# Interleaving the second attention, and spreading recurrence, routing and row sums over the first, in a four-block transformer kernel

## The chip, the cores and the metric

The kernel runs on one core of one Trainium2 chip. The metric is the device time of one execution in microseconds (us), lower is better. A core has five engines with a program order of their own: PE (TensorE: matmul, with its weight loads as PEld), DVE (VectorE), ACT (ScalarE), POOL (GpSimd) and SP (SyncE); they wait for one another through semaphores. SBUF is the on-chip memory, PSUM the eight banks of 128 x 512 f32 into which PE writes.

## The reference, cut to what matters

X holds 32 sequences of 128 tokens of width 128. Two layers of four sub-blocks run over it; all arithmetic that matters here is f32.

```python
# layer 0
h = x * modulation(cond)                       # modulated
x = x + attention(h, 16 heads of 64, causal) @ W_out
F, I = sigmoid(x @ W_f), sigmoid(x @ W_i)      # recurrence
C = x @ W_h + b_h
f, i = F / (F + I + eps), I / (F + I + eps)
F = scan_t(f * state + i * C)
for cyc in range(3):                           # twist
    th = (0.3*a*tanh-ish gate(F)) + 0.7*a*gate_of_mean
    F = F + th * twist(F)                      # twist(F): F's four quarters permuted, signs changed
x = x + F
# layer 1
gate  = top2(softmax(segment_means(x) ...))    # routed
x = x + experts picked by gate, and a shared one
x = layernorm(x + attention(x, 16 heads of 8, key mask, causal))
x = x + slots(lowrank(x))
```

The two attentions are softmax(Q K^T + mask) V for every sequence and head. The gate th is the same for all 128 rows of one token, so twist(F + th * twist(F)) = twist(F) + th * twist(twist(F)) and twist(twist(F)) = -F.

## The kernel before, in words

X stays in SBUF, transposed (width on the partitions, 4096 token columns), in eight chunks g of 512 columns (CB = 4 sequences of S = 128). `ps()` takes one of the eight PSUM banks, `mm` (L268), `tt` (L279) and `act` (L339) issue a matmul, a two-input elementwise operation on the engine named, and an activation; many groups of the profile therefore carry these helpers' lines and are told apart by their tiles. PE and ACT execute in the order of the program text. For DVE and POOL a list scheduler decides the order.

**First stage (up to about 650 us).** The loop `for h in range(NH + 1)` runs over 16 half-chunks (8 heads of a chunk each) and, inside, over four sequences b. Every (h, b) is one *unit*, pushed on `pipe = Staggered(0, 3, 4, 5)`: on each push the scores of this unit, the transposes of the unit three pushes back, the values of the one four back and, for the last sequence, the output projection of the one five back are issued.

- `scores` (L408 to L434): mask and Q K^T for 8 heads into two banks; a DVE maximum for each bank (L426), 8 exponentials on ACT into `s_sb`, a DVE sum over 128 x 1024 (L431, `s_sum`), its reciprocal (L432), and the normalisation of `s_sb` on POOL (L279).
- `turned` (transposes L441; copies `pT` on ACT and on DVE L443), `values` (copy `oT` on DVE L453), `projected` (adds to X on DVE).

Between the pushes stand, in program order: three pieces of `projections(h + 1)` for each b (Q, K and V of the next half-chunk); `modulated(g + 1)` ahead of the first push of odd h (xs on POOL, one matmul, `hT` on DVE); `recurrence(g)`, all of it after the push at b = 0 of odd h from 3; `twisted(g0, cyc)` after the push at b = 0 of h = 6, 7, 8, 10, 11, 12, 14, 15, 16 (one cycle each of a pair of chunks, in four steps with a projection piece or a push between them); `routed(g0)`, driven to its end at once after the push at b = 3 of h = 8 and 12; and `prepared()`, low-rank and constant preparation for the last sub-block, ahead of the twist at h = 6.

- `recurrence` (L457 to L497): three matmuls with X; F and I by sigmoid on ACT, C on DVE (L480); R = 1 / (F + I + eps) on DVE (L481, L482); products on DVE and POOL; L486; eight scans (L490, L491), POOL product, one scan of 512 columns (L495).
- `twisted` (L500 to L572): three small matmuls with Gelu, then in `fourth` tanh on ACT, L563 on DVE, the matmul `twist` x F, th * twist on DVE, F + th on DVE for the first chunk and on POOL for the second; in cycle 2 X + F on POOL.
- `routed` (L575 to L646): sums of X over segments (DVE), gate matmuls, softmax and top-2 as a chain of some 25 small DVE operations and one exponential on ACT, ending in `r_wd` (L279), a matmul with ones, and the expert rows for the gathers.

**Second stage (about 650 to 1301 us), and a drain.** Four turns r of 32 pieces: 24 expert pieces, then eight attention pushes (two chunks). A dictionary `plan` ties other steps to piece numbers: `last_recurrence` at 2, the twist of the last pair of chunks at 7, 13 and 19, `routed(4)` at 24 and `routed(6)` at 26 of turn 0, and the slot sub-block of the turn before. Expert weights are gathered by indirect DMAs issued from POOL (L786). One attention push issues, through `pipe = Staggered(0, 1, 2, 3, 4)`, in this order: scores(n), weights(n-1), turned(n-2), values(n-3), normed(n-4). For one sequence `weights` are four DVE maxima (L862) and 16 exponentials `s` on ACT for four banks of four heads (hg = 0 to 3), `turned` are 16 transposes (L873) with one copy `p1T` per bank, on DVE (L877) for hg = 0 and 2 and on ACT for 1 and 3, and `values` are 16 matmuls and an ACT copy `oS`.

Of the kernel before, what the change touches and what calls it, by code (L numbers as in the profile page):

```python
# [11 lines left out]
F32 = mybir.dt.float32  # L12
# [227 lines left out]
def program(ctx, tc, out, xT, packs, where):  # L240
# [102 lines left out]
    with (  # L343
# [62 lines left out]
        def unit(h, b):  # L406
# [8 lines left out]
            def scores():  # L415
                two = [ps(), ps()]
                for par in range(2):
                    mm(two[par], ident16, outer(causal16, 4), stop=False)
                for i in range(4):
                    for par in range(2):  # L420
                        r = slice(64 * par, 64 * par + 64)
                        mm(two[par][:, bass.ts(i, S)], qks[h][2 * i][r, cs], qks[h][2 * i + 1][r, cs], start=False, stop=(i == 3))
                s = pool.tile([P, 8, S], F32, tag="s_sb", name="s_sb", bufs=5)
                nm = pool.tile([P, 8], F32, tag="s_max", name="s_max", bufs=5)
                for par in range(2):
                    V.tensor_reduce(nm[:, 4 * par : 4 * par + 4], b3(two[par]), AX.X, ALU.max, negate=True)  # L426
# [4 lines left out]
                V.tensor_reduce(sm, s, AX.X, ALU.add)  # L431
                V.reciprocal(sm, sm)  # L432
                tt(G, s, s, inner(sm, S), ALU.mult)
                at["s"] = s  # L434
# [32 lines left out]
        def recurrence(g, three):  # L467
# [11 lines left out]
            mm(p, w("w_h"), col(g))  # L479
            V.tensor_scalar(C, p, w("b_h"), None, ALU.add)  # L480
            V.scalar_tensor_tensor(R, F, 1e-8, I, ALU.add, ALU.add)  # L481
            V.reciprocal(R, R)  # L482
            tt(V, F, F, R, ALU.mult)
            tt(G, I, I, R, ALU.mult)
            tt(G, I, I, C, ALU.mult)
            V.tensor_scalar(F, F, 1e-8, None, ALU.add)  # L486

            for b in range(CB):
# [4 lines left out]
                )  # L493
            tt(G, I, I, R, ALU.mult)
            V.tensor_tensor_scan(F, w("reset"), I, 0.0, ALU.mult, ALU.add)  # L495
            tt(V, F, F, C, ALU.add)
            Fs[g] = F  # L497


        def twisted(g0, cyc):  # L500

# [52 lines left out]
            def fourth():  # L554
# [4 lines left out]
                for k, g in enumerate(gs):  # L559
                    th = mpool.tile([P, CH], F32, tag="th", name="th")  # L560
                    act(th, two[k], AF.Tanh, bias=hb4, scale=0.5)
                    cB = cBs[g0][:, k * CB : (k + 1) * CB]
                    V.scalar_tensor_tensor(b3(th), b3(th), ar3, inner(cB, S), ALU.mult, ALU.add)  # L563
                    p = ps()
                    mm(p, w("twist"), Fs[g])
                    tt(V, th, th, p, ALU.mult)
                    tt(G if k else V, Fs[g], Fs[g], th, ALU.add)
                    if cyc == 2:
                        tt(G, col(g), col(g), Fs[g], ALU.add)
# [7 lines left out]
        def routed(g0):  # L577
# [14 lines left out]
            V.tensor_scalar(agg[:, 0, :], agg[:, 0, :], 1.0 / S, None, ALU.mult)  # L592
            V.tensor_scalar(agg[:, 1:3, :], agg[:, 1:3, :], 1.0 / (S - LH), None, ALU.mult)
            p = ps()
            for k in range(3):
# [42 lines left out]
            wd = rt([nb, 4, nb], "wd")  # L638
            tt(V, wd, inner(pick, nb), outer(ident[:nb, :nb], 4), ALU.mult)
            p = ps()  # L640
            mm(p[:, : 4 * nb], ones[:nb, :], wd.rearrange("p e b -> p (e b)"))
# [71 lines left out]
        for piece in projections(0):  # L713
            piece()
        pipe = Staggered(0, 3, 4, 5)
        for h in range(NH + 1):


            pieces = []
            if h + 1 < NH:  # L720
                if h % 2:
                    modulated(h // 2 + 1)
                pieces = projections(h + 1)
# [27 lines left out]
    with tc.tile_pool(name="l1", bufs=1) as pool:  # L751
# [87 lines left out]
        def attention(g, b):  # L839
# [16 lines left out]

            def weights():
                four = at["p"]
                s = pool.tile([P, 16, S], F32, tag="s1", name="s1", bufs=2)
                nm = pool.tile([P, 16], F32, tag="s1max", name="s1max", bufs=2)  # L860
                for hg in range(4):
                    V.tensor_reduce(nm[:, bass.ts(hg, 4)], b3(four[hg]), AX.X, ALU.max, negate=True)  # L862
                    for j in range(4):
                        h = 4 * hg + j
                        act(s[:, h, :], four[hg][:, bass.ts(j, S)], AF.Exp, bias=nm[:, h : h + 1])
                at["s"] = s

            def turned():
                pT = pool.tile([P, 16, S], F32, tag="p1T", name="p1T", bufs=2)
                for hg in range(4):  # L870
                    p = ps()
                    for j in range(4):
                        T.transpose(p[:, bass.ts(j, S)], at["s"][:, 4 * hg + j, :], ident)  # L873
                    if hg % 2:
                        act(pT[:, bass.ts(hg, 4)], b3(p), AF.Copy)
                    else:
                        V.tensor_copy(pT[:, bass.ts(hg, 4)], b3(p))  # L877
                at["pT"] = pT

# [273 lines left out]
        def last_recurrence():  # L1153
            three = [pool.tile([P, CH], F32, tag=t, name="rec", bufs=2) for t in ("qT", "kT", "R")]
            recurrence(NCH - 1, three)

# [15 lines left out]
        at(26, routed, NCH - 2)  # L1172
        steps_of = {}

        def twisted_steps(cyc):
            if cyc not in steps_of:
                steps_of[cyc] = twisted(NCH - 2, cyc)
            return steps_of[cyc]

        for r in range(NP):  # L1180
# [18 lines left out]
            at(t + 30, slots_told, c)  # L1199
        pipe = Staggered(0, 1, 2, 3, 4)  # L1200
        running = []
        for i in range(END + 2 * TURN):
# [7 lines left out]
            if k < 3 and 1 <= r <= NP:  # L1210
                pipe.push()
            for gen in list(running):
# [6 lines left out]
            if k >= 24 and r < NP:  # L1219
                b = k - 24  # L1220
                pipe.push(*attention(2 * r + b // CB, b % CB))
                if k == TURN - 1:
                    pipe.push()

# [29 lines left out]
```

## Time and profile before

| what | value |
|---|---|
| three runs of before | 1384.09, 1378.07, 1384.84 us; median 1384.09 |
| the profiled execution | 1384.86 us, of which the span of the trace is 1383.1 |
| mean granted TensorE clock | 0.943 |
| PE busy, first attention (40 to 640 us) | 554.75 of 600 us |
| PE busy, second stage (778 to 1301 us) | 468.15 of 523 us |
| PE busy, drain (1301 to 1383 us) | 52.90 of 82 us, clock 0.66 |
| largest group on POOL | s_sb normalisation, 64 x 1917 ns |
| ACT_TABLE_LOAD | 59 x 1283 ns |

The page gives, for one execution, how long each engine was busy, the span in 40 slices (a digit 9 means busy for 90% or more; PEclk is the granted TensorE clock in tenths), and groups of equal instructions with their number, busy time, mean duration and the idle time ahead of them with the engine and tile that ended it. A timeline line has start, length, engine, line, operation, `out<-in` by tile name, shapes and number; a bracket at its end is the engine's idle time before it and what ended it. Matmuls are pipelined, so a busy PE isn't a PE at its peak. An f32 matmul appears as two records.

### The profile page before, as it was taken

To read this page: it belongs to the slowest core of one execution; us is meant where nothing else is said; L and a number is where in the kernel's file an instruction comes from. 1 tells how busy PE (TensorE), PEld (TensorE's weight loads), DVE (VectorE), ACT (ScalarE), POOL (GpSimd) and SP (SyncE) were. 2 spreads that over 40 slices of the span, in tenths; PEclk is the share of its full clock that TensorE was granted. 3 is DMA by queue.
4 is the path that set the end of the run, shared out by engine and by line. 5 is a ranking of instruction groups with operands and counts; after the bars stand their busy time and mean duration, and the time that the engine had idled before them with its cause. 6 is when DMAs were issued, how large, how long until landed. Compare 5 with 4: busy or idle time off the path is not lost. (4 is left out here: it accounts for less than half of the span.)

```text
span 1383.1 us, 20674 instructions
## 1 busy us (share of the span) xinstructions
PE 1206.7 (87%) x7743; PEld 720.2 (52%) x7743; DVE 784.5 (57%) x1862; ACT 782.7 (57%) x2044; POOL 334.0 (24%) x292
## 2 busy tenths in 40 slices
PE   4999999997999979978788789899899889989856
PEld 1565655444554545544445356655567456665633
DVE  1657684666757567574423764466644755456743
ACT  2765654654565645642554674668546774658521
POOL 1323231322322223222433111321023110311000
PEclk9999999998999999998999799999999999999975
DMA  6000000000000000000424002320044001310000
GB/s 241 1 1 1 1 1 0 1 1 1 1 1 1 1 1 1 1 1 0 155 69 127 12 1 70 120 87 1 9 146 128 11 1 50 121 35 1 12 5 16
DMA packets 15987, 49.67 MB, mean 36 GB/s; under 512 B 1424, under 2 KB 5648, under 8 KB 15504
## 3 DMA queue, kind: packets, MB, share of 16 engines
q0 software_dynamic: 9504, 40.01, 9.1%
q1 hardware_dynamic: 5808, 7.29, 1.5%
q8 instruction: 61, 1.00, 0.3%
q10 hardware_dynamic: 576, 1.05, 0.2%
q14 instruction: 38, 0.31, 0.1%
HBM read 46.25 MB, written 2.10 MB: 35 GB/s over the span
## 5 line engine op out<-in xcount | busy, mean ns | idle before, releaser
L339 ACT ACTIVATE s_sb<-ps,s_max 128x128 f32<-128x128 f32 x512 | 139.2, 383 | 127.1 <-DVE s_max L426 123.8
L279 POOL TENSOR_TENSOR s_sb<-s_sb,s_sum 128x1024 f32<-128x1024 f32 x64 | 122.7, 1917 | 275.2 <-DVE s_sum L432 183.3
L268 PE MATMUL ps<-hT,w_attn 128*128 128x512 f32 x256 | 128.9, 627 | 16.3 <-DVE hT L279 11.8
L339 ACT ACTIVATE s<-ps,s1max 128x128 f32<-128x128 f32 x512 | 134.2, 404 | 1.0 <-DVE s1max L862 1.0
L426 DVE TENSOR_REDUCE s_max<-ps 128x4 f32<-128x512 f32 x128 | 82.2, 680 | 68.0 <-PE ps L268 67.8
L339 ACT ACTIVATE he<-ps,ew 128x128 f32<-128x128 f32 x256 | 72.6, 369 | 63.3 <-issue 29.1
L862 DVE TENSOR_REDUCE s1max<-ps 128x4 f32<-128x512 f32 x128 | 81.8, 681 | 36.2 <-PE ps L268 36.1
L339 ACT ACT_TABLE_LOAD x59 | 75.7, 1283 | 44.5 <-PE ps L268 23.5
L339 ACT ACTIVATE qk<-ps 128x512 f32<-128x512 f32 x128 | 74.8, 627 | 42.3 <-PE ps L268 41.7
L786 POOL DMA_INDIRECT ew<-in_expert,rows x64 | 62.7, 980 | 136.3 <-DVE ye L796 131.3
L431 DVE TENSOR_REDUCE s_sum<-s_sb 128x8 f32<-128x1024 f32 x64 | 77.8, 1216 | 23.7 <-ACT s_sb L339 23.6
L268 PE MATMUL ps<-he,ew 128*128 128x128 f32 x512 | 79.1, 294 | 13.6 <-ACT he L339 11.0
L268 PEld LDWEIGHTS ps<-he,ew 128*128 128x128 f32 x512 | 68.8, 195 | 31.4 <-ACT he L339 29.1
L796 DVE SCALAR_TENSOR_TENSOR ye<-ps,ew 128x128 f32<-128x128 f32 x64 | 22.4, 350 | 107.2 <-PE ps L268 107.2
L268 PEld LDWEIGHTS ps<-hT,w_attn 128*128 128x128 f32 x256 | 45.2, 193 | 69.9 <-issue 40.3
L268 PEld LDWEIGHTS ps<-qk 64*128 64x128 f32 x1024 | 64.6, 194 | 31.4 <-issue 31.4
L268 PE MATMUL ps<-qk 64*128 64x128 f32 x1024 | 77.2, 292 | 0.0
L873 PEld LDWEIGHTS ps<-w_base,s 128*128 128x128 f32 x512 | 59.8, 149 | 32.6 <-ACT s L339 20.4
L873 PE MATMUL ps<-w_base,s 128*128 128x128 f32 x512 | 71.6, 290 | 4.2 <-ACT s L339 4.2
L268 PE MATMUL ps<-pT,v 128*64 128x128 f32 x1024 | 72.5, 285 | 3.0 <-DVE pT L443 2.1
L441 PE MATMUL ps<-w_base,s_sb 128*128 128x128 f32 x512 | 72.1, 285 | 2.8 <-DVE th L279 1.7
L268 PE MATMUL ps<-X,ew 128*128 128x128 f32 x512 | 70.9, 278 | 0.0
(295 smaller groups left out, 2286.9 us busy)
## 6 DMA issues: line engine op xcount, KB each, us to landing
w_attn<-in_attn POOLq DMA_DIRECT2D x2, 1024.0 KB, 10.5
out_x<-ot SPq DMA_DIRECT2D x8, 256.0 KB, 2.3
X<-in_xT ACTq DMA_DIRECT2D x4, 256.0 KB, 7.4
X<-in_xT SPq DMA_DIRECT2D x4, 256.0 KB, 9.5
w_lowr<-in_lowr SPq DMA_DIRECT2D x1, 1024.0 KB, 12.5
ew<-in_expert,rows POOLq DMA_INDIRECT x64, 4.5
w_ffn<-in_ffn SPq DMA_DIRECT2D x1, 928.0 KB, 10.4
w_mix<-in_mix SPq DMA_DIRECT2D x1, 800.0 KB, 11.5
```

The costliest lines, as they stand in the source:

```text
L268: T.matmul(out_, lhsT=lhsT, rhs=rhs, start=start, stop=stop)
L279: eng.tensor_tensor(out_, a, b, op)
L339: return tc.keep_in_program_order(A.activation(*args, **kwargs))
L426: V.tensor_reduce(nm[:, 4 * par : 4 * par + 4], b3(two[par]), AX.X, ALU.max, negate=True)
L431: V.tensor_reduce(sm, s, AX.X, ALU.add)
L441: T.transpose(p[:, bass.ts(i, S)], at["s"][:, 4 * par + i, :], ident)
L786: G.indirect_dma_start(ew, None, table, bass.IndirectOffsetOnAxis(ap=rows[:, r, k : k + 1], axis=0))
L796: V.scalar_tensor_tensor(t, y, ew[:, 1028:1029], ew[:, 1029:EW], ALU.add, ALU.mult)
L862: V.tensor_reduce(nm[:, bass.ts(hg, 4)], b3(four[hg]), AX.X, ALU.max, negate=True)
L873: T.transpose(p[:, bass.ts(j, S)], at["s"][:, 4 * hg + j, :], ident)
```

## The change: what it does

1. *Row sums* (L431): POOL adds the two halves of each row of 128 (128 x 512), then the two quarters of that (128 x 256), and DVE sums what is left (32 columns per head, 256 in all, for 1024).
2. *Recurrence in steps*: `recurrence` becomes a generator of five parts; it is begun after the push at b = 1 (was 0), and each later push runs one part. C is an ACT Identity with bias (was DVE). The reciprocal is taken in two halves.
3. *Twist carried along*: the matmul `twist` x F is issued in cycle 0 only. For the cycles after, `turned[k]` holds twist(F), updated as twist(F) - th * F: the product v on POOL, the subtraction on DVE in cycle 0 and on POOL in cycle 1. The twist steps begin at b = 2 (was 0).
4. *Routing in steps*: three more yields in `routed`, and in the first stage one part is run per push, from b = 3 of h = 8 and 12.
5. *Moved*: `prepared()` from h = 6, b = 0 to h = 16, b = 2; `modulated(g + 1)` from ahead of odd h to after the first push of the even h before it.
6. *Second attention*: `weights` and `turned` take the bank hg as argument, and one push issues, for hg = 0 to 3, weights(n-1, hg) and turned(n-2, hg), then values(n-3), scores(n), normed(n-4). In turn 0 the two carried tiles lie in a tile of `s1`.

```diff
-                V.tensor_reduce(sm, s, AX.X, ALU.add)
+                half = pool.tile([P, 8, 64], F32, tag="s_half", name="s_half")
+                tt(G, half, s[:, :, 0:64], s[:, :, 64:128], ALU.add)
+                tt(G, half[:, :, 0:32], half[:, :, 0:32], half[:, :, 32:64], ALU.add)
+                V.tensor_reduce(sm, half[:, :, 0:32], AX.X, ALU.add)
...
-            V.tensor_scalar(C, p, w("b_h"), None, ALU.add)
+            act(C, p, AF.Identity, bias=w("b_h"))
+            yield
             V.scalar_tensor_tensor(R, F, 1e-8, I, ALU.add, ALU.add)
-            V.reciprocal(R, R)
+            for k in range(2):
+                V.reciprocal(R[:, bass.ts(k, CH // 2)], R[:, bass.ts(k, CH // 2)])
+            yield
...
-                    p = ps()
-                    mm(p, w("twist"), Fs[g])
-                    tt(V, th, th, p, ALU.mult)
-                    tt(G if k else V, Fs[g], Fs[g], th, ALU.add)
+                    F, TF = Fs[g], turned[k]
+                    if cyc == 0:
+                        p = ps()
+                        mm(p, w("twist"), F)
+                        TF = p
+                    if cyc < 2:
+                        v = mpool.tile([P, CH], F32, tag="h1", name="v")
+                        tt(G, v, th, F, ALU.mult)
+                    tt(V, th, th, TF, ALU.mult)
+                    tt(G if k else V, F, F, th, ALU.add)
+                    if cyc < 2:
+                        tt(V if cyc == 0 else G, turned[k], TF, v, ALU.subtract)
...
-                if h % 2:
-                    modulated(h // 2 + 1)
...
-                if b == 0 and 3 <= h < NH and h % 2 == 1:
-                    recurrence((h - 3) // 2, [pool.tile([P, CH], F32, tag="rec%d" % i, name="rec", bufs=1) for i in range(3)])
+                for gen in list(running):
+                    if next(gen, gen) is gen:
+                        running.remove(gen)
+                if b == 1 and 3 <= h < NH and h % 2 == 1:
+                    gen = recurrence((h - 3) // 2, [pool.tile([P, CH], F32, tag="rec%d" % i, name="rec", bufs=1) for i in range(3)])
+                    next(gen)
+                    running.append(gen)
+                if b == 0 and h % 2 == 0 and h + 2 < NH:
+                    modulated(h // 2 + 1)
...
-                if b == 0 and k >= 0 and k % 4 < 3:
-                    if k == 0:
+                if b == 2 and k >= 0 and k % 4 < 3:
+                    if k % 4 == 0:
+                        turned = [pool.tile([P, CH], F32, tag="tw%d" % i, name="tw", bufs=1) for i in range(2)]
+                    work = twisted(2 * (k // 4), k % 4, turned)
+                    if h == NH:
                         prepared()
-                    work = twisted(2 * (k // 4), k % 4)
                 if b == 3 and 0 <= k < NH - 6 and k % 4 == 2:
-                    for _ in routed(2 * (k // 4)):
-                        pass
+                    running.append(routed(2 * (k // 4)))
...
-        pipe = Staggered(0, 1, 2, 3, 4)
+        def advance(item=None):
+            line.append(item)
+            w1, t1, v1, n1 = (line[-k] if k <= len(line) else None for k in (2, 3, 4, 5))
+            for hg in range(4):
+                if w1:
+                    w1[1](hg)
+                if t1:
+                    t1[2](hg)
+            if v1:
+                v1[3]()
+            if item:
+                item[0]()
+            if n1:
+                n1[4]()
```

More of the change, by code (lines that the diff above doesn't have):

```diff
@@ L486, in recurrence @@
             V.tensor_scalar(F, F, 1e-8, None, ALU.add)
+            yield
             for b in range(CB):
@@ L494, in recurrence @@
             tt(G, I, I, R, ALU.mult)
+            yield
             V.tensor_tensor_scan(F, w("reset"), I, 0.0, ALU.mult, ALU.add)
@@ L497, in recurrence, with twisted @@
             Fs[g] = F
-        def twisted(g0, cyc):
+        def twisted(g0, cyc, turned):
             gs = (g0, g0 + 1)
@@ L593, in routed @@
             V.tensor_scalar(agg[:, 1:3, :], agg[:, 1:3, :], 1.0 / (S - LH), None, ALU.mult)
+            yield
             p = ps()
@@ L639, in routed @@
             tt(V, wd, inner(pick, nb), outer(ident[:nb, :nb], 4), ALU.mult)
+            yield
+            yield
             p = ps()
@@ L715, in program @@
         pipe = Staggered(0, 3, 4, 5)
+        turned = {}
+        running = []
         for h in range(NH + 1):
-            pieces = []
-            if h + 1 < NH:
-                if h % 2:
-                    modulated(h // 2 + 1)
-                pieces = projections(h + 1)
+            pieces = projections(h + 1) if h + 1 < NH else []
             for b in range(CB):
@@ L855, in scores, with weights, turned @@
                 at["p"] = four
[L857 to L878, printed above, removed]
+            def weights(hg):
+                p = at["p"][hg]
+                if hg == 0:
+                    at["s"] = pool.tile([P, 16, S], F32, tag="s1", name="s1", bufs=2)
+                    at["nm"] = pool.tile([P, 16], F32, tag="s1max", name="s1max", bufs=2)
+                V.tensor_reduce(at["nm"][:, bass.ts(hg, 4)], b3(p), AX.X, ALU.max, negate=True)
+                for j in range(4):
+                    h = 4 * hg + j
+                    act(at["s"][:, h, :], p[:, bass.ts(j, S)], AF.Exp, bias=at["nm"][:, h : h + 1])
+            def turned(hg):
+                if hg == 0:
+                    at["pT"] = pool.tile([P, 16, S], F32, tag="p1T", name="p1T", bufs=2)
+                p = ps()
+                for j in range(4):
+                    T.transpose(p[:, bass.ts(j, S)], at["s"][:, 4 * hg + j, :], ident)
+                if hg % 2:
+                    act(at["pT"][:, bass.ts(hg, 4)], b3(p), AF.Copy)
+                else:
+                    V.tensor_copy(at["pT"][:, bass.ts(hg, 4)], b3(p))
             def values():
@@ L1154, in last_recurrence @@
             three = [pool.tile([P, CH], F32, tag=t, name="rec", bufs=2) for t in ("qT", "kT", "R")]
-            recurrence(NCH - 1, three)
+            return recurrence(NCH - 1, three)
         TURN, NP = 24 + 2 * CB, NCH // 2
@@ L1172, in program @@
         at(26, routed, NCH - 2)
-        steps_of = {}
+        steps_of, last_turned = {}, []
         def twisted_steps(cyc):
+            if cyc == 0 and cyc not in steps_of:
+                t = pool.tile([P, 16, S], F32, tag="s1", name="tw", bufs=2).rearrange("p h s -> p (h s)")
+                last_turned.extend([t[:, 0:CH], t[:, CH : 2 * CH]])
             if cyc not in steps_of:
-                steps_of[cyc] = twisted(NCH - 2, cyc)
+                steps_of[cyc] = twisted(NCH - 2, cyc, last_turned)
             return steps_of[cyc]
@@ L1199, in program @@
             at(t + 30, slots_told, c)
-        pipe = Staggered(0, 1, 2, 3, 4)
+        line = []
+        def advance(item=None):
[12 more added lines that the diff above has]
+                n1[4]()
         running = []
@@ L1210, in program @@
             if k < 3 and 1 <= r <= NP:
-                pipe.push()
+                advance()
             for gen in list(running):
@@ L1220, in program @@
                 b = k - 24
-                pipe.push(*attention(2 * r + b // CB, b % CB))
+                advance(attention(2 * r + b // CB, b % CB))
                 if k == TURN - 1:
-                    pipe.push()
+                    advance()
 def build(inputs):
```

## The prediction

> **What bounds the kernel now.** I read the page first: engine shares, then busy tenths in 40 slices.
>
> ```profile
> span 1383.1 us, 20674 instructions
> PE 1206.7 (87%) x7743; PEld 720.2 (52%) x7743; DVE 784.5 (57%) x1862; ACT 782.7 (57%) x2044; POOL 334.0 (24%) x292
> ...
> PE   4999999997999979978788789899899889989856
> ...
> PEclk9999999998999999998999799999999999999975
> ```
>
> TensorE is busy for 87% and near full in most slices, so time can be won in three ways only: fewer matmuls, fewer PE stalls, or fewer stretches at the half clock. The stretches of busy time (columns: length; PE, PEld, DVE, ACT, POOL busy; granted clock; DMA) say where the room is.
>
> ```profile
> 40.00:640.00 600.00, 554.75 (x3395) 306.73 (x3392) 387.63 (x638) 347.55 (x854) 176.44 (x104) 0.96 0.00 1
> 336.00:342.00 6.00, 2.24 (x4) 1.33 (x5) 3.28 (x23) 0.20 (x1) 0.26 (x1) 0.50 0.01 3
> 914.00:974.00 60.00, 53.90 (x468) 29.64 (x470) 41.20 (x86) 46.79 (x155) 10.57 (x12) 1.00 0.01 2
> ```
>
> In the first attention (40 to 640) PE lacks 45 us of 600; POOL, with 176 us, has room. 914 to 974 is one block of second attention, with PE busy for 54 us of 60. Next, a plain unit of the first attention in the timeline, since every unit's row sums change:
>
> ```profile
> 154.98 1.29 DVE L426 TENSOR_REDUCE s_max<-ps 128x4 f32<-128x512 f32 x2 [3.41 <-PE ps L268]
> 155.77 2.17 ACT L339 ACTIVATE s_sb<-ps,s_max 128x128 f32<-128x128 f32 x8 [1.71 <-DVE s_max L426]
> ...
> 157.97 1.22 DVE L431 TENSOR_REDUCE s_sum<-s_sb 128x8 f32<-128x1024 f32 x1 [0.23 <-ACT s_sb L339]
> ...
> 159.22 0.20 DVE L432 RECIPROCAL s_sum<-s_sum 128x8 f32<-128x8 f32 x1
> ...
> 159.96 1.90 POOL L279 TENSOR_TENSOR s_sb<-s_sb,s_sum 128x1024 f32<-128x1024 f32 x1 [8.24 <-PE ps L268]
> ...
> 161.33 0.69 DVE L426 TENSOR_REDUCE s_max<-ps 128x4 f32<-128x512 f32 x1 [1.90 <-PE ps L268]
> ```
>
> The mask matmuls of neighbouring units stand at 153.26 and 159.61: one unit is 6.35 us with PE back to back, and DVE waits for PE (3.41 and 1.90 us). The stalls lie in the units that carry more. The waits of PE and the timeline name them:
>
> ```profile
> PE ps L268 <- DVE r_wd L279: 21.4, 4, 7.7
> ...
> PE ps L268 <- DVE th L279: 6.0, 5, 1.9
> ...
> PE ps L268 <- DVE X L279: 5.2, 6, 0.9
> ```
>
> ```profile
> 339.76 0.60 PE L268 MATMUL ps<-r_wd,w_base 8*128 8x32 f32 x2 [7.72 <-DVE r_wd L279]
> ```
>
> Routing stalls PE for 7.72 us twice in the first attention and 5.73 us once in turn 0; the recurrence waits 0.87 us six times for the add to X. Last, one step of the second attention on ACT:
>
> ```profile
> 1101.62 4.22 ACT L339 ACTIVATE s<-ps,s1max 128x128 f32<-128x128 f32 x16
> 1105.61 0.72 ACT L339 ACTIVATE p1T<-ps 128x512 f32<-128x512 f32 x1
> 1106.59 0.60 ACT L339 ACTIVATE p1T<-ps 128x512 f32<-128x512 f32 x1 [0.26 <-PE ps L873]
> 1107.63 0.60 ACT L339 ACTIVATE oS<-ps 128x512 f32<-128x512 f32 x1 [0.44 <-PE ps L268]
> ```
>
> ACT works 6.1 us of a step of about 7 (16 exponentials, two copies, one copy of values) and sits idle for 0.7 us between its copies, behind transposes that stand after all the exponentials.
>
> **What the Trainium skill says.** "TensorE: Matmul & The Clock Gate", What's actually happening: the PE clock falls to half after an idle window of about 3.4 us. The trace agrees: clock 0.50 in 336 to 342, in the 7.72 us stall. "GPSIMD Engine Reference", 3.1 Elementwise: a GpSimd tensor_tensor of 2048 columns takes 4497 ns, so 512 would be near 1.1 us; this trace has 1.27 us (X<-X,F, 128x512), which I use. The same page, 8. Key points: GpSimd shares an SBUF interface with VectorE. The trace's F<-F,th add (1265/1593/1657 ns at minimum, median and maximum) fits such contention, and I let a half sum cost 1.27 to 1.65.
>
> **The change, part by part**, against the profiled run: 1384.86 us, 1.8 outside the span, 0.8 above the median of 1384.09.
>
> 1. *Twist carried along.* 16 of 24 twist matmuls go. Each is two records of 0.43 us spacing (two passes of 512 columns), so 0.86 us on a full PE: 16 × 0.86 = 13.7; 12 lie in the first attention (−10.3), 4 in turn 0, where PE has gaps (−2 instead of −3.4). Added: per pair two v products and a cycle-1 subtraction on POOL for each chunk (1.27 to 1.65 each), cycle-0 subtractions on DVE (0.69). None feeds the next PE step but through F+th, so 0, except in point 6.
>
> 2. *Routing in steps.* The 7.72 us stalls go twice (−15.4). After each, the clock stays at half up to 348, clock 0.84 in 342 to 348; estimate 2.5 us per stall, so −5. Turn 0: −5.7. Next late is the agg reduction, two units of work earlier: nothing. Sum −20 and −6.
>
> 3. *Recurrence from b = 1, in steps.* Its matmuls no longer stand behind the X add of the same push: 0.87 × 6 = −5, and 0.7 more where I see its twin (1.11 us at 134) → −6. C goes to ACT (8 × 0.69), where ACT's share is 58% of this stretch: 0.
>
> 4. *Modulated early; twist away from recurrence.* Units at odd h, b = 2 take 8.6 us against 6.35 + 0.86 for the modulated matmul: 1.4 × 4 = 5.6. Units h = 7 and 11, b = 1 (twist meets recurrence) take 10.05 and 9.97 against 7.2: 5.6. The stalls at h = 15 (1.49, 1.68, 1.07) may remain; −12 with 1 of these. With fewer stalls, fewer half-clock windows: those at 231, 293, 385, 460, 515, 552 are 30 us, cost up to 15; I take −6 (0 to −12).
>
> 5. *prepared moved.* Unit h = 6, b = 0 takes 26.2 us against 17.7 for a twist unit: −8.5. At h = 16 its 32 matmuls (3.76 us) and its ah and xab waits (0.38, 1.26) return in a stretch with stalls: +7.5. Net −1. It issues no DMA; on POOL and SP nothing moves past it.
>
> 6. *Row sums halved on POOL.* Per unit DVE loses 1.22 − 0.41 (estimate from 0.68 for 512 elements) = 0.8, 51 us over 64 units, all beside PE: 0. POOL gains 1.27 to 1.65 (half) and 0.7 to 0.9 (quarter, estimate: half the columns plus its fixed part). The DVE reduction now waits for POOL, and behind it stands the next s_max. In the unit shown: exponentials end 157.94, + 0.05 + 1.35 + 0.75 + 0.1 → 160.2, reduction and reciprocal to 160.9, s_max due at 161.33: 0.4 us of cover. With the upper ends it is 0.2 us late, and twist units have DVE filled (cycle 0 has 3 us more). Bounds 0 and +25 (64 × 0.4); a gain is excluded only while DVE has 1.9 us idle. I take +8.
>
> First attention: −10.3 − 20 − 6 − 12 − 6 − 1 + 8 = −47.
>
> 7. *Second attention interleaved.* Transposes of an older step stand between exponentials, so ACT's copies find them done: the 0.26 + 0.44 us go, and PE's waits for p1T (9.4 us in all) with them. A step then has ACT's 6.1 + 0.2. Before: the first six steps of a block are 6.27 to 7.53 us apart, mean 6.83; so −0.5 × 32 = −16; the loop exponentials, values, masks, maximum (I add these to 6.3) leaves no more. Turn ends see other limits; I take −14, bounds 0 and −25. Cover lost: values(n) wait for group 1's exponentials in the same push through a PSUM bank.
>
> 8. *POOL in turn 0*: v, subtraction and F add (1.3 to 1.65 each) stand between issues of expert gathers (0.98 us each): 8 × 1.5 = 12 us on POOL, busy 43 of 118. Bounds 0 and +6; I take +2. Three more table loads (page count of 59 at 1.28 us): "ScalarE: Activation LUTs", What ACT_TABLE_LOAD costs, gives about 1.28 too: +3.8 of ACT beside PE, 0.
>
> Second stage: −2 − 6 − 14 + 2 = −20. Sum −67: 1384.9 − 67 = **1318 us**.
>
> **The rivals.** (a) *DVE waits for POOL eat the gain*: point 6 at its upper end (+25) and no clock gain (4): −67 + 17 + 6 = −44, and routing's tail still late in part (+4): about 1345. For: POOL's latency stands in DVE's queue. Against: 1.9 us of DVE idle per unit. (b) *Interleave gives nothing*: the new PSUM wait replaces the old: −67 + 14 → 1332; with 0.2 us more per step, 1338. For: exponentials of the next push still depend on scores behind values. (c) *More gain*: steps at 6.1 us (−24 in point 7), half clock gone (−12), 6 at 0: −67 − 10 − 6 − 8 → 1294. (d) *Slower*: POOL becomes the bound of the first attention. Its loop per unit is half + quarter + the reduction's round trip + normalise = 1.65 + 0.9 + 0.9 + 1.9 = 5.35 us, if POOL takes the units strictly one after the other; it decides from 6.35. Were the halves, which read with a stride, to take 3 and 1.9 us, the loop is 7.7 to 8: 1.65 × 64 = +105 − 67 → 1422. Against: 1.27 us is measured for the same number of elements. (e) *The change doesn't act*, since DVE and POOL order is a scheduler's: the built order shows the transposes between exponentials and the routing steps between units; only point 6's placement is open.
>
> **Chances.** Forecast 1318 (1300 to 1335): 0.52; (b) and (a), 1332 to 1365: 0.24; (c) 0.13; between 1365 and 1377: 0.02; within 0.5% (1377 to 1391), which is about what a measurement can tell from no change: 0.03; (d) 0.06. The range takes (a), (b) and most of (c): 1282 to 1362. Faster 0.91, same 0.03, slower 0.06.
>
> **What would show it.** Right: no PE wait for r_wd near 7 us; 4657 instead of 4673 matmul instructions in the program and 64 F,w_mix records for 96; plain units still at 6.35; no clock of 0.50 at the former routing; steps of the second attention at 6.3; half sums at 1.3 to 1.65 us. Wrong: s_max waiting for s_sum or POOL in each unit; half sums above 2 us; ACT idle in second attention with waits on PE values; a PE wait for ah or xab over 3 us at the end of the first attention.

## The result, and the profile after

The changed kernel takes 1376.74 us (median of 19 runs, 1370.38 to 1380.87), the kernel before 1383.65 (19 runs, 1377.44 to 1388.80): a ratio of 0.9952, 95% interval 0.9936 to 0.9969. The forecast was 1318 with a range from 1282 to 1362. The change is worth 7 us, not 67, and the time lies outside the range. The profiled execution spans 1375.8 us.

The page of after, engine shares and the slices of PE, POOL and the clock:

```profile
span 1375.8 us, 20779 instructions
...
PE 1190.6 (87%) x7711; PEld 721.4 (52%) x7711; DVE 759.2 (55%) x1870; ACT 782.6 (57%) x2055; POOL 495.4 (36%) x444
...
PE   4999898979898998977787889898899989998865
...
POOL 1655655465555555552544311221023110311100
PEclk9999999989999899978899999999999899999876
```

PE did lose 16 us of busy time (1206.7 to 1190.6), and DVE 25, but the span fell by 7.3 only, and POOL went from 334 to 495 us. PE stands still elsewhere: its waits in after are

```profile
PE ps L268 <- ACT h L339: 28.1, 19, 8.3
...
PE ps L268 <- DVE pT L446: 13.9, 5, 3.6
```

The wait for r_wd (21.4 us before) is gone from this list, as forecast, and that for X fell from 5.2 to 0.4. In its place PE waits 28.1 us for the twist's h (8.2 before) and 13.9 for pT (2.8 before). Both stand behind the softmax maxima: h behind exponentials on ACT, these behind s_max on DVE, and pT behind s_max on DVE itself. At 282.83 us, for instance, PE has stood still for 4.69 us: ACT waits 4.34 us for s_max, loads a function table (1.28 us), does the exponentials and one copy, loads a table again (1.28 us), and only then forms h. Two stretches show where the time went, the first attention up to the scores of its last unit, and from there to the first scores of the second attention. (The columns are those of the stretches shown for before.) After:

```profile
40.00:613.00 573.00, 528.01 (x3240) 291.02 (x3239) 348.88 (x617) 341.41 (x845) 316.58 (x241) 0.96 0.00 1
613.00:768.00 155.00, 121.57 (x592) 75.72 (x591) 65.42 (x122) 67.55 (x142) 66.21 (x69) 0.88 0.25 78
```

Before, the same two pieces of work:

```profile
40.00:620.00 580.00, 536.89 (x3300) 298.12 (x3298) 378.30 (x623) 338.01 (x835) 170.75 (x101) 0.97 0.00 1
620.00:761.00 141.00, 117.34 (x576) 68.62 (x572) 55.35 (x111) 65.97 (x143) 51.71 (x57) 0.93 0.27 87
```

The first attention gained 7 us, where the forecast had it gain 47 up to the end of the stage; the stretch after it, which holds the preparation, the drain and turn 0's experts, became 14 us longer at a clock of 0.88. Turn 0's attention gave 13 us back.

The groups of after that carry the added work (line, engine, form, number; busy us, mean ns; idle before and who ended it):

```profile
L279 POOL TENSOR_TENSOR s_half<-s_sb 128x512 f32<-128x512 f32 x64 | 82.5, 1289 | 117.1 <-ACT s_sb L339 116.9
L279 POOL TENSOR_TENSOR s_half<-s_half 128x256 f32<-128x256 f32 x64 | 48.8, 763 | 4.9
L268 PE MATMUL ps<-F,w_mix 128*128 128x512 f32 x64 | 33.6, 641 | 0.0
L434 DVE TENSOR_REDUCE s_sum<-s_half 128x8 f32<-128x256 f32 x64 | 26.6, 416 | 132.6 <-POOL s_half L279 132.6
L279 POOL TENSOR_TENSOR v<-th,F 128x512 f32<-128x512 f32 x16 | 23.8, 1517 | 45.7 <-DVE th L571 45.7
L485 DVE SCALAR_TENSOR_TENSOR rec<-F,rec 128x512 f32<-128x512 f32 x8 | 17.0, 2120 | 12.4 <-ACT rec L339 12.4
```

The durations were forecast well (1289 and 763 ns for 1.27 to 1.65 and 0.7 to 0.9; 416 for 0.41; 64 records for 96). What the forecast didn't have is the last line: a DVE sum of 128 x 512 that took 684 ns before takes 2120.

### The profile page after: what moved, and what is told of

Read it like the earlier page. It is cut to its first block, busy times and chain, and to the rows that moved or that the text cites. A ratio compares the mean times of both kernels' runs of the same rounds, so it can differ in the third digit from the quotient of the medians.

```text
span 1375.8 us, 20779 instructions
## 1 busy us (share of the span) xinstructions
PE 1190.6 (87%) x7711; PEld 721.4 (52%) x7711; DVE 759.2 (55%) x1870; ACT 782.6 (57%) x2055; POOL 495.4 (36%) x444
## 5 line engine op out<-in xcount | busy, mean ns | idle before, releaser
L339 ACT ACTIVATE s<-ps,s1max 128x128 f32<-128x128 f32 x512 | 138.1, 399 | 8.0 <-DVE s1max L888 8.0
L279 POOL TENSOR_TENSOR s_half<-s_sb 128x512 f32<-128x512 f32 x64 | 82.5, 1289 | 117.1 <-ACT s_sb L339 116.9
L434 DVE TENSOR_REDUCE s_sum<-s_half 128x8 f32<-128x256 f32 x64 | 26.6, 416 | 132.6 <-POOL s_half L279 132.6
L268 PE MATMUL ps<-he,ew 128*128 128x128 f32 x512 | 82.2, 302 | 12.1 <-ACT he L339 11.2
L268 PEld LDWEIGHTS ps<-he,ew 128*128 128x128 f32 x512 | 72.3, 205 | 30.1 <-ACT he L339 27.4
L279 POOL TENSOR_TENSOR km<-kT,w_base 128x512 f32<-128x512 f32 x32 | 34.4, 1074 | 132.9 <-PE ps L268 103.4
## 6 DMA issues: line engine op xcount, KB each, us to landing
w_ffn<-in_ffn SPq DMA_DIRECT2D x1, 928.0 KB, 10.2
```

The lines of the kernel that those rows point to most:

```text
L268: T.matmul(out_, lhsT=lhsT, rhs=rhs, start=start, stop=stop)
L279: eng.tensor_tensor(out_, a, b, op)
L339: return tc.keep_in_program_order(A.activation(*args, **kwargs))
L434: V.tensor_reduce(sm, half[:, :, 0:32], AX.X, ALU.add)
```

## The experiments

Three theories. **A**: recurrence parts and carried twist put work that waits for POOL into DVE's in-order queue ahead of the maxima. **B**: POOL's added load by itself. **C**: the parts are worth what was forecast and stalls at other places, with the half clock after them, give the gain back. (Where a text that was put on record before its run names a rival by a letter, the letter is that text's own.) All ratios are to the kernel before; a point is 1% of its time, 13.8 us.

**Undoing one part of the change each.**

Full row sums:

```diff
-                tt(G, half, s[:, :, 0:64], s[:, :, 64:128], ALU.add)
-                tt(G, half[:, :, 0:32], half[:, :, 0:32], half[:, :, 32:64], ALU.add)
-                V.tensor_reduce(sm, half[:, :, 0:32], AX.X, ALU.add)
+                V.tensor_reduce(sm, s, AX.X, ALU.add)
```

> The changed kernel with the DVE row sums of before (128x1024 on DVE, nothing on POOL for them); all else as changed. Theory A (the time went into DVE's in-order queue: recurrence parts and twist products that wait for POOL stand ahead of s_max; the halves only add to it): 1365 to 1380 us, POOL busy falls from 495 to about 360 us, the PE stalls at 278, 441, 597 and 620 us remain at over 2 us each. Rival B (POOL's added load is the cause by itself): near the forecast, 1320 to 1350 us, and these stalls are gone.

Measured: 1355.21 us, 0.9798 (0.9772 to 0.9823), 1.5 points under after. Between the theories: the halves cost 21 us, more than A and less than B gave them.

A twist matmul in every cycle:

```diff
-                    F, TF = Fs[g], turned[k]
-                    if cyc == 0:
...
+                    p = ps()
+                    mm(p, w("twist"), Fs[g])
+                    tt(V, th, th, p, ALU.mult)
+                    tt(G if k else V, Fs[g], Fs[g], th, ALU.add)
```

> The changed kernel with the twist matmul in every cycle, as before (16 more matmuls of 0.86 us, no v product, no carried tile). Theory A: th may not be overwritten by th*TF until POOL has read it for v, so the carried form costs stalls of 2.8, 2.8 and 5.7 us (at 297, 460, 620) plus half clock after them; these go, the matmuls come back: 1368 to 1380 us, about no change. Rival B (the carry is worth its 13.7 us of matmul): 1388 to 1394 us.

Measured: 1349.02 us, 0.9754 (0.9729 to 0.9780). Both theories missed: the carry, which removes 13.7 us of matmul, costs 27 us net (some of it through the clock in turns that it doesn't touch, see below).

Recurrence in one go, as before (with C on DVE, the reciprocal in one piece and no steps inside; the diff shows the call alone):

```diff
-                if b == 1 and 3 <= h < NH and h % 2 == 1:
-                    gen = recurrence(...)
+                if b == 0 and 3 <= h < NH and h % 2 == 1:
+                    recurrence(...)
```

> The changed kernel with the recurrence of before: in one go after the push at b = 0 of odd h, C on DVE, one reciprocal; twist still from b = 2, routing in steps. Theory A (recurrence in steps puts reciprocals, scans and waits for POOL ahead of the maxima of four pushes): stalls of about 4.7 us for the twist's h at b = 2 of h = 7, 11, 15 and of 1.7 to 3.6 us at b = 0 of even h go, the 0.87 us waits for X return: 1350 to 1366 us. Rival B (the steps gain 6 us as forecast and the stalls come from POOL): 1380 to 1395 us.

Measured: 1411.44 us, 1.0199 (1.0173 to 1.0224), 35 us above after. Theory A is wrong on the recurrence: its steps are a gain, and while POOL is loaded a larger one than the 24 us that steps 3 and 4 of the forecast gave them together with the moves. All of it lies in the first attention.

The second attention of before:

```diff
-            for hg in range(4):
-                if w1:
-                    w1[1](hg)
-                if t1:
-                    t1[2](hg)
...
+        pipe = Staggered(0, 1, 2, 3, 4)
```

> The changed kernel with the second attention of before (scores, weights, turned, values in one block each). If the interleave gains its 14 us: 1386 to 1394 us. If its shorter steps (6.0 for 6.5 us between exponentials) are given back in half clock (54 for 32 us between turn 0's attention and the drain): 1374 to 1382 us.

Measured: 1388.50 us, 1.0046 (1.0026 to 1.0066), 0.94 points above after: 13 us, the forecast's 14. ACT in one block of after shows how:

```profile
928.11 2.08 ACT L339 ACTIVATE s<-ps,s1max 128x128 f32<-128x128 f32 x8
930.10 0.57 ACT L339 ACTIVATE p1T<-ps 128x512 f32<-128x512 f32 x1
930.58 2.09 ACT L339 ACTIVATE s<-ps,s1max 128x128 f32<-128x128 f32 x8
932.57 0.57 ACT L339 ACTIVATE p1T<-ps 128x512 f32<-128x512 f32 x1
933.05 0.57 ACT L339 ACTIVATE oS<-ps 128x512 f32<-128x512 f32 x1
933.52 0.49 ACT L339 ACTIVATE sl_s<-sl_s 128x128 f32<-128x128 f32 x2
934.17 2.17 ACT L339 ACTIVATE s<-ps,s1max 128x128 f32<-128x128 f32 x8 [0.16 <-DVE s1max L888]
```

Each copy of p1T now follows a group of eight exponentials and has no wait in front; this step is 934.17 - 928.11 = 6.06 us. But the 13 us aren't spread over the turns as the forecast had them. From its first maxima to those of the next turn, turn 0 takes 152.6 us here and 142.4 in after. Turns 1 and 2 take 158.8 and 158.7 here, 157.6 and 160.6 in after, and 153.1 and 153.3 with two parts undone (the next run). So the interleave is worth over 5 us in each of these turns too where the clock stays up, and after lost that to the half clock.

**Two undone at once, a freed carry, routing alone.**

> The changed kernel with the DVE row sums of before and with the twist matmul in every cycle: recurrence and routing in steps, the moves and the interleave remain. If the two costs are separate (21.5 and 27.7 us, from the two runs that undid one each): 1376.7 - 49 = 1328, 1320 to 1336 us, near the forecast. If both act through the same thing (POOL's load slowing DVE), so that undoing one takes most of the other: 1340 to 1350 us.

Full sums and twist matmuls together, in the changed kernel: 1335.22 us, 0.9677 (0.9646 to 0.9708). Undoing both gives 2.75 points, 1.54 and 1.98 each: mostly separate, with a shared part of 0.8 points (11 us).

The freed carry keeps the matmuls away and lets DVE go on without POOL:

```diff
-                    tt(V, th, th, TF, ALU.mult)
-                    tt(G if k else V, F, F, th, ALU.add)
+                    up = mpool.tile([P, CH], F32, tag=("h2", "h3")[k], name="up", bufs=1) if cyc < 2 else th
+                    tt(V, up, th, TF, ALU.mult)
+                    if cyc == 0:
+                        V.tensor_copy(turned[k], TF)
+                    tt(G if k or cyc < 2 else V, F, F, up, ALU.add)
```

> The changed kernel; in twist cycles 0 and 1 th*TF goes to a tile of its own, the sum F + th*TF is on POOL for both chunks, twist(F) is copied out of PSUM on DVE in cycle 0 and the subtraction is always on POOL, so DVE never waits for POOL's v product. Theory A (the carry costs by DVE waiting for POOL before it may overwrite th and F): the stalls of 2.8 us at 297 and 460 and of 5.7 us at 620 go while the 13.7 us of matmul stay away: 1335 to 1355 us. Rival C (it costs by POOL's load and by slowed DVE operations beside it): 1368 to 1380 us.

1369.72 us, 0.9912 (0.9889 to 0.9935), 0.4 points under after. That is within what its text gave the rival, POOL's load and slowed operations. But up to the last unit's scores it won 10 us (603.0 for 613.1), and by turn 0's attention it had lost 5 of them again: its tile shares a buffer with the values of attention_inputs, for which DVE waits 4.6 us there until POOL has read it, and PE stands still for 6.44 us at that place. The freed carry takes away DVE's waits for v; seven of its th products are still slowed beside POOL, to as much as 1.8 us. So it doesn't tell A from B cleanly.

Routing in steps alone, on the kernel before (with the three more yields in `routed`; the diff shows the call alone):

```diff
-                    for _ in routed(2 * (k // 4)):
-                        pass
+                    running.append(routed(2 * (k // 4)))
```

> The kernel before with routing in steps alone (the generator's three added yields, one part per push in the first attention). Forecast's step 2: the two 7.72 us stalls, the 5.73 us one and the half clock after them go: 1384 - 26 = 1358, 1352 to 1366 us. Rival (the small DVE operations come late elsewhere): 1370 to 1384 us.

1362.67 us, 0.9862 (0.9838 to 0.9887): 19 us. The half-chunks h = 8 and 12 lose 10.4 and 10.0 us, as forecast; a little comes back at h = 10 and 14 (1.7 us each).

> As the first of these four, with the preparation put back to h = 6. Forecast's step 5: net 1 us, so within 4 us of the first. If it costs more in the drain of the first attention, where stalls and half clock surround it (10.2 us of half clock at 617 to 628 in the run with full sums): 4 to 10 us less than the first.

1338.06 us, 0.9692 (0.9664 to 0.9721): the intervals of this run and of the first overlap, so moving the preparation is worth nothing that these runs resolve (forecast: -1).

**Load or wait?** In the first kernel POOL forms halves and quarters that nobody reads, in the second it does the carry's products on constants (`tt(G, v, w("reset"), w("reset"), ALU.mult)`); in the third the carry's product is on DVE (`tt(V, v, th, F, ALU.mult)`); in the fourth a `yield` parts the halves of the reciprocal.

> The run with both undone (1335 us), and POOL still forms the halves and quarters of every unit, but nobody reads them: DVE sums the whole row as before. POOL's load and its traffic on SBUF beside DVE are then those of the halved sums, the wait of DVE's s_sum for POOL is not there. If load and slowed DVE operations (the rec sum at 2.3 us for 0.7) are what the halved sums cost: 1346 to 1354 us. If the wait in DVE's queue is: 1333 to 1339 us.

1345.44 us, 0.9739 (0.9703 to 0.9776): +9 us over 1335 of the 11 that the halves cost in this setting (0.9754 against 0.9677), with intervals that just touch (0.9646 to 0.9708 and 0.9703 to 0.9776). By the medians it is load, for most. Up to the last unit's scores the profile is 10.7 us longer than with both undone, and 6.1 of these stand after the pushes at b = 3 of h = 3, 5, 9 and 13: at h = 9 PE's stall there grows from 0.79 to 2.44 us, and ahead of it on DVE the recurrence's F + eps, with one SBUF operand, takes 1.38 us beside a half sum for 0.43 without one.

> The run with both undone (1335 us: twist matmul in every cycle), and POOL also does the carry's products in cycles 0 and 1 and its subtractions in cycle 1, on constants, nobody reading them. The carry's load on POOL without its waits. If the load is what the carry costs (the run with the carry and DVE sums had 1355): 1348 to 1358 us. If the waits of th and F for POOL are: 1333 to 1340 us.

1343.01 us (1335.99 to 1346.77), 0.9704 (0.9671 to 0.9736): +4 us, with intervals that overlap. Inconclusive, though less than the carry's 17 (0.9798, 0.9772 to 0.9823, against 0.9677). But the idle products wait for no gate, so they don't fall beside the twist's operations on DVE: no th product and no F+th is slowed in this run.

> The run with DVE sums and the carry (1355 us), with the product v = th*F on DVE instead of POOL: DVE gets 16 products of 0.7 us more, and th and F wait for no POOL operation; only the cycle 1 subtractions stay on POOL. If waiting for POOL inside DVE's queue is the cost: the block from the gate to the next maximum falls from 6.5 to about 5 us, 1338 to 1346 us. If it is any longer DVE block: 1350 to 1357 us.

1348.39 us, 0.9745 (0.9716 to 0.9774): between the two expectations; 7 of the 17 us come back, with intervals that just touch. This is net of the 16 products that DVE now does itself (0.7 us each). And the four sums F+th beside POOL's subtraction are still slowed. So the wait for POOL's product isn't the whole cost, and the run doesn't say how the rest divides.

> The run with both undone, with the two halves of the recurrence's reciprocal (1.7 us each) run in two successive pushes instead of one. If what is left at h = 7, 11 and 15 (PE waits of 4.7 to 5.3 us for the twist's h, behind exponentials that wait for maxima behind the reciprocals) comes from the 3.4 us block: 1322 to 1331 us. If the scans or the sum ahead decide: 1333 to 1338 us.

1335.31 us, 0.9655 (0.9625 to 0.9684): no change that is clear.

**Where the carry costs.** `carried = g0 < 4` in the first kernel, `g0 >= 4` in the second, with a matmul in every cycle elsewhere.

> DVE row sums, the twist carried for chunks 0 to 3 only (h = 6 to 12), a matmul in every cycle for chunks 4 to 7. If the carry costs only where PE has no projection matmuls to cover it: 1331 to 1339 us, as without any carry (1335). If it costs the same in each carried cycle: half of 20 us, 1343 to 1349 us.

1342.78 us, 0.9683 (0.9656 to 0.9710): by ratio as without a carry, by time between the two expectations.

> The complement: the twist carried for chunks 4 to 7 only (h = 14 to 16 and turn 0). If the carry costs only there: 1350 to 1358 us, as with the carry everywhere (1355). If the same in each carried cycle: 1343 to 1349 us.

1348.49 us, 0.9734 (0.9708 to 0.9761): +0.6 points, 8 us; by the time alone that is what was expected of an even cost, so the place is read from the profiles. There the stretch from the last unit's scores to turn 0's scores is 146.7 us without a carry, 145.0 with it in the first pairs, 155.2 in the last pairs and 159.8 in all. With full sums the place is clear; the size in the total (8 here, 17 for all) is not fully accounted for, since these kernels also differ by up to 10 us in turns 1 and 2, which the carry doesn't touch (see the clock, below).

**The parts alone on the kernel before.**

> The kernel before with the row sums halved on POOL alone. Forecast's step 6: +8, 1388 to 1396 us. By the run with idle halves (+10) and the one with the halves and twist matmuls (+14): 1392 to 1402 us. If the halves cost only together with the recurrence in steps: 1380 to 1387 us.

1393.07 us, 1.0056 (1.0034 to 1.0078): +8, the forecast's own number. The DVE sum that takes 2120 ns in after takes 686 ns here, so it has no part in these 8 us; how they come about isn't shown.

> The kernel before with the twist carried along alone (twist still after b = 0, recurrence in one go, routing at once). Forecast's step 1: -12, 1368 to 1376 us. If the carry's longer DVE block costs by itself in the drain of the first attention and in turn 0: 1384 to 1400 us.

1396.09 us, 1.0097 (1.0067 to 1.0127): +13 where -12 was forecast. The sign was wrong, without any other part of the change. The loss lies in the first attention, at h = 6, 7, 11 and 15: the last unit's scores come at 634.8 us for 620.5. In this kernel, at h = 7, on DVE:

```profile
281.48 2.30 DVE L495 TENSOR_TENSOR_SCAN F<-w_mix,rec 128x512 f32<-128x512 f32 x1 [1.16 <-POOL rec L279]
283.70 0.72 DVE L563 SCALAR_TENSOR_TENSOR th<-th,ar,cB 128x512 f32<-128x512 f32 x1
284.35 0.68 DVE L279 TENSOR_TENSOR F<-F,rec 128x512 f32<-128x512 f32 x1
284.95 2.38 DVE L279 TENSOR_TENSOR th<-th,tw 128x512 f32<-128x512 f32 x2
287.25 1.75 DVE L279 TENSOR_TENSOR F<-F,th 128x512 f32<-128x512 f32 x1
288.92 1.27 DVE L426 TENSOR_REDUCE s_max<-ps 128x4 f32<-128x512 f32 x2
```

on POOL:

```profile
284.50 1.68 POOL L279 TENSOR_TENSOR v<-th,F 128x512 f32<-128x512 f32 x1 [1.80 <-DVE th L563]
286.81 1.65 POOL L279 TENSOR_TENSOR tw<-tw,v 128x512 f32<-128x512 f32 x1 [0.63 <-DVE th L279]
```

and on PE:

```profile
290.85 1.18 PE L268 MATMUL ps<-causal,ident 128*128 128x512 bf16 x2 [6.89 <-DVE pT L443]
```

From 283.70 on DVE isn't idle in these lines: it is slowed. The first of the two th products begins while POOL forms v (284.50 to 286.18), takes 1.78 of the 2.38 us and ends 0.55 us after v; F+th takes 1.75 us beside POOL's subtraction (0.68 before, at the same place); and the scan ahead of them, beside the other chunk's v (281.41 to 282.70), takes 2.30 for 1.23. That is 3.2 us, and the unit grows by 3.4 (10.0 to 13.4). The maximum comes at 288.92, and PE waits 6.89 us where the kernel before waited 1.93. Two matmuls of 0.86 us were saved for that.

> The same with the halved row sums (which alone took +8). If the two costs are separate: 8 us above the run with the carry alone. If POOL's load makes them more than their sum: 14 us or more above it.

1416.25 us, 1.0250 (1.0215 to 1.0285). The parts alone give 0.56 + 0.97 = 1.53 points; together they take 2.50. So the parts don't add, but most of the missing point, 13 us, isn't made where POOL carries both. The spans of the profiles differ by 22.2 us from the carry alone, where the halves alone added 9.3. Of the 13 between, 1 lies in the first attention, 6 from the last unit's scores to turn 0's (the last half sum is formed 9 us into that stretch; half clock 31 us, for 21 with the carry alone and 17 with the halves alone), 3 in turn 0's attention and 3 in turns 1 and 2, which neither part touches. DVE's waits for v are 5.9 us in both runs. What moves the stalls after the halves have ended is open.

**What is left at h = 7, 11 and 15.**

```diff
-                if b == 1 and 3 <= h < NH and h % 2 == 1:
+                if b == (3 if h % 4 == 3 and h > 3 else 1) and 3 <= h < NH and h % 2 == 1:
```

> The run with both undone (1335 us), and the recurrence begun at b = 3 instead of 1 in h = 7, 11 and 15, after the twist of b = 2. If its sums and reciprocals, and its table loads, are what holds back the exponentials and the twist's Gelu behind them (PE stalls of 3.5 to 5.3 us and the half clock after them): 1318 to 1328 us. If the stalls move with it: 1333 to 1340 us.

1328.92 us, 0.9615 (0.9586 to 0.9644), 8.6 us under the run that it builds on, and the fastest of all: it beats both kernels. PE's wait for the twist's h was, with the recurrence at b = 1 everywhere,

```profile
PE ps L268 <- ACT h L339: 22.6, 19, 5.3
```

and with it behind the twist

```profile
PE ps L268 <- ACT h L339: 14.7, 19, 2.3
```

## Why the prediction was wrong

| step of the forecast | forecast us | measured us (from) |
|---|---|---|
| 1 twist carried along | -12 | +13 alone on before; +17 with full sums and +27 in the changed kernel, of which 10 and 11 lie in turns 1 and 2, which it doesn't touch |
| 2 routing in steps | -26 | -19 (alone on before) |
| 3, 4 recurrence, moves, clock | -24 | about -12 (what is left of -45, both undone, after 2 and 7, if the parts add) |
| 5 preparation moved | -1 | not resolved |
| 6 halved row sums | +8 | +8 alone on before; +11 with twist matmuls; +21 in the changed kernel |
| 7 interleave | -14 | -13 |
| 8 POOL in turn 0 | +2 | part of 1 |

**Step 1 failed, and in its sign.** It said of the added products: "None feeds the next PE step but through F+th, so 0". True of the data, not of the queue: DVE runs in order, and the next unit's s_max stands behind the carry's operations. Two things lengthen these. th is overwritten in place, so DVE waits until POOL has read it for v. In after:

```profile
DVE th L279 <- POOL v L279: 9.5, 8, 1.2
```

And an operation of DVE that runs beside one of POOL is slowed. Both stand in cycle 1 of h = 7 of after:

```profile
291.23 1.41 DVE L571 SCALAR_TENSOR_TENSOR th<-th,ar,cB 128x512 f32<-128x512 f32 x2 [0.76 <-ACT th L339]
293.83 2.37 DVE L279 TENSOR_TENSOR th<-th,tw 128x512 f32<-128x512 f32 x2 [1.19 <-POOL v L279]
296.13 1.75 DVE L279 TENSOR_TENSOR F<-F,th 128x512 f32<-128x512 f32 x1
297.80 1.28 DVE L426 TENSOR_REDUCE s_max<-ps 128x4 f32<-128x512 f32 x2
```

DVE waits 1.19 us for v; the first th product takes 1.77 us beside the other chunk's v, and F+th 1.75 us beside POOL's subtraction. s_max begins 6.57 us after the gate's operations. Over the whole kernel the waits are 9.5 us, and the four th products and four sums F+th that are slowed take 8.6 us more than alone. The variants divide the 17 us with full sums only in part: 7 go when the product leaves POOL, and the products' bare load measured 4 (not resolved). The rest isn't divided; the slowed sums F+th are in it. Where the carry costs depends on what else stands in the queue: with full sums in the drain at h = 15 and in cycle 1 of turn 0, where PE has no projection matmuls to do meanwhile (in after a stall of 5.67 us for pT and one of 3.12 for the experts' hid), and alone on the kernel before, where twist and recurrence follow the same push, in the first attention.

**Step 6 was right alone and wrong beside the rest.** The +8 was picked between bounds of 0 and +25, so that it came true so closely is in part luck. Its 0.4 us of cover was counted for a plain unit, and a plain unit did stay at 6.35 us. What was left out is that POOL's added 131 us would meet DVE operations on SBUF operands, those of the recurrence in steps above all. On DVE, in after:

```profile
270.48 2.32 DVE L485 SCALAR_TENSOR_TENSOR rec<-F,rec 128x512 f32<-128x512 f32 x1 [0.27 <-ACT rec L339]
272.83 3.37 DVE L487 RECIPROCAL rec<-rec 128x256 f32<-128x256 f32 x2
```

and on POOL:

```profile
270.36 1.90 POOL L279 TENSOR_TENSOR s_sb<-s_sb,s_sum 128x1024 f32<-128x1024 f32 x1 [0.83 <-DVE s_sum L435]
```

The DVE sum starts beside POOL's normalisation and ends 0.54 us after it, as if it had to let POOL finish. The same sum is shorter where less of POOL's operation is left when it starts (1.08 and 1.45 us with both undone), and its end comes at the same distance. With the halves undone its mean is 949 ns instead of 2120, with the halves idle 1161. So the slowed sum is one part of the cost in after; the idle halves cost mostly elsewhere, after b = 3 of odd h, as shown above. The prediction cited the Trainium skill, "GPSIMD Engine Reference", 8. Key points, for this sharing and used it for POOL's side only (1.27 to 1.65); the page names VectorE operations with two SBUF inputs, and the trace shows the price on their side: 684 ns alone, 2120 on the mean in after.

**Steps 3 and 4** had the right sign (undoing the steps costs 35 us in the changed kernel) and were too large: the recurrence, one push ahead of the twist in h = 7, 11 and 15, puts its sum and reciprocal ahead of s_max, and ACT, in program order, puts the exponentials ahead of the twist's Gelu. Two table loads of 1.28 us stand in that chain as well (the stall at 282.83); the prediction put the three that the change adds at 0, as beside PE. Moving the recurrence behind the twist gives 8.6 us of the 12 that are missing. **Steps 2 and 7** held in the main (-19 for -26, -13 for -14), and so did the signs named for them: no wait for r_wd near 7 us, no half clock at the old places of the routing, 6.06 us for the step shown of the second attention. But the sum for step 7 agrees in part by luck: turn 0 gave 10 us of it, and turns 1 and 2 gave nothing. Rival (a), late DVE for POOL, named the mechanism of 6 and gave it 1345; that the carry adds to it was in no rival. Of the three theories, A holds for the carry in part and not for the recurrence, B holds, by the medians, for most of the halves, and C for what the clock took.

**The clock.** The time at half clock rose from 161 to 189 us in after, where step 4 had it fall; the run with both undone has 120. Part of that is not a part of the change at all. Turns 1 and 2 issue the same work in after and in the run with both undone. After (turn 1, turn 2):

```profile
909.00:1067.00 158.00, 140.54 (x1037) 95.52 (x1035) 87.18 (x271) 98.50 (x284) 33.42 (x38) 0.96 0.21 64
1067.00:1227.00 160.00, 143.72 (x1029) 95.47 (x1028) 86.79 (x270) 98.30 (x283) 28.66 (x33) 0.93 0.15 45
```

With both undone:

```profile
879.00:1032.00 153.00, 135.39 (x1034) 90.80 (x1032) 86.73 (x271) 98.37 (x284) 33.49 (x38) 0.99 0.21 66
1032.00:1185.00 153.00, 135.47 (x1032) 91.36 (x1031) 86.49 (x270) 98.48 (x283) 28.73 (x33) 0.99 0.15 47
```

The same work takes 12 us longer, at a clock of 0.96 and 0.93 for 0.99. Over the profiles with the interleave, turn 1 (from its first scores to those of turn 2) takes 153.1 to 153.5 us with 3.4 us at half clock, 156.2 with 10.2 and 157.6 with 13.7, and nothing between. The traces tie which of these a kernel gets to how its stalls fall against the clock's windows. All half-clock stretches of a profile begin on one grid of 3.41 us. The gap of 1.94 us with which a turn's second attention begins falls across an edge of it in turn 1 of after (0.73 and 1.21 us of idle PE on the two sides), and the clock stays up; in turns 2 and 3 it falls into one window nearly whole (1.84 and 1.94 us), and half clock follows, for 13.7 and for 3.4 us; why so unlike is open. No run moved a stall along the grid on purpose. The clock makes 12 of the 42 us between the spans of after and of the run with both undone; 19 lie in the first attention up to the last unit, 9 from there to turn 0's scores, 3 from those to turn 1's. It is also in the sizes of the carry: turns 1 and 2 hold 11 of the 29.7 us between the spans of after and of the run with twist matmuls, and 10 of the 20.9 between full sums and both undone. In the kernel before and in that with the carry alone both turns take 158.7 us, so +13 is the clean figure.

## What to carry to other kernels

Work taken off the bounding engine is worth its time only if what replaces it stays out of the in-order queue that feeds that engine. List, for every operation added on a helper engine, which tile it still reads when the next instruction of the feeding engine wants to write it, and which operations of the feeding engine will run beside it. Don't add up the prices of parts that were measured one by one: +8 and +13 became +34. And before a difference is put down to an edit, compare stretches that the edit doesn't touch; here they differ by 12 us through the granted clock.

## What the runs showed of the hardware

- A half-clock stretch needs no long stall. In after, a PE gap of 1.29 us at 861 is followed by 3.4 us at half clock at 864. The prediction rested on the Trainium skill's idle window of about 3.4 us ("TensorE: Matmul & The Clock Gate", What's actually happening). The stretches do come in multiples of 3.41 us and begin on one grid, but the measurements decide against a window that is idle throughout. Divided along that grid, from 40 us on, the 20 profiles have 230 windows at full clock with 2 us or more of idle PE, and half clock followed 228 of them; it followed 23 of 6089 with under 1.2 us, and 158 of the 556 between. Once at half clock, 0.6 us of idle PE in a window kept it there (290 of 291 windows). Idle PE is counted from the profile's records, whose ends are modelled.
- An elementwise DVE operation with two SBUF operands of 128 x 512 that began while a POOL tensor_tensor had more than 0.1 us to go ended 0.55 us after that one, in all 21 cases of after: it took 0.99 to 2.34 us, by how much of POOL's operation was left, for 0.67 to 0.69 alone. Small operations were held in the same way: one of the routing on 8 x 16 elements took 1.79 us for 0.15. Where DVE began first, it kept its time (0.67 to 0.75 us) and POOL's operation was longer (v took 1.72 to 1.75 us for 1.27). DVE reductions out of PSUM (s_max, 674 to 679 ns) and copies out of PSUM (pT, 0.67 to 0.69 us) didn't change.
